# A two-layer graph network: one gather in eight waits for the second last one, and layer 2's dense terms are added a layer earlier

## The chip, the cores and the metric

The kernel runs on one core of a Trainium2 chip. A core has four compute engines with queues of their own: TensorE (PE, matrix products, with PEld for the loading of the stationary operand), VectorE (DVE), ScalarE (ACT) and GpSimd (POOL). SyncE (SP) issues plain transfers. Gathers, that is transfers whose source rows are given by a list of indices, are issued from POOL's queue. The metric is the device time of one execution in microseconds.

## The reference

The graph has 12,500 nodes with 128 features each and 200,000 edges, sorted by the node they end in. An edge's relation is the argmax of 10 of its 42 attributes. A layer takes, for every node and relation, the mean of the features of the source nodes, multiplies it by the relation's 128 x 128 matrix, sums over the relations, and adds the node's own features times a root matrix and a bias. Two such layers, with a relu between them, are followed by the residual and a layer norm:

```python
def _rgcn_layer(x, src, dst, edge_type, w_rel, root, bias):
    seg = dst * NUM_REL + edge_type
    xs = x[src]
    sums = jax.ops.segment_sum(xs, seg, num_segments=N * NUM_REL)
    cnt = jax.ops.segment_sum(jnp.ones(seg.shape, x.dtype), seg, num_segments=N * NUM_REL)
    mean = (sums / jnp.maximum(cnt, 1.0)[:, None]).reshape(N, NUM_REL, -1)
    return jnp.einsum('nrd,rdo->no', mean, w_rel) + x @ root + bias
h = jax.nn.relu(_rgcn_layer(x, src, dst, edge_type, w_rel1, root1, b1))
x = _layernorm(x + _rgcn_layer(h, src, dst, edge_type, w_rel2, root2, b2), axis=-1)
```

## The kernel before

The edges are cut into 1563 tiles of 128. For a tile, one gather (`gather`, L506 to L517) reads the 128 source rows from device memory into one sixteenth of the tile `g`: from `x` in layer 1, from `hD`, the hidden rows that layer 1 has stored, in layer 2. So a layer has 1563 gathers, the two layers 3126, and nothing else stands in POOL's queue once the constants are made. Sixteen tiles make a group, and `g` has three buffers, so gathers can be three groups ahead of their use. Towards the end of a layer the groups get smaller.

For each group, `ones` writes on DVE a matrix of zeros and weights per tile (`oh`, L531): its 120 columns are the 10 relations times 12 neighbouring end nodes, and a weight is one over the edge count of that node and relation. `sums` (L547) multiplies the gathered rows by it on PE into `zp` (L555); ACT moves the result to `zs` (L570). In full groups the first product of a group waits for all the group's gathers at once ("one wait per group"). `project` (L575) multiplies by the 10 relation matrices (L582). `add` (L593) spreads the result over 160 node columns (L598) and adds it on DVE into `acc` (L604), which holds 128 features x all nodes. `layer` (L606) is the loop over the groups: the projection stands one group, the addition two groups behind.

The nodes are cut into 29 blocks: 24 of 512, then smaller ones. When the groups have gone far enough that a block gets no more edges, its `finish` runs. In layer 1 that is `hidden` (L439): `block_in` (L402) has loaded the block's rows of `x` on SP's queue and transposed them (PE L415, ACT L417); `block_rows` (L422) forms in PSUM the root product (L427) plus the accumulator turned back to rows (L428), and writes layer 2's bias into the block's columns of `acc` (L430); then comes the relu and the store of the rows to `hD`. In layer 2 it is `final` (L449): `block_in` loads the block's rows of `x` and of `hD`, transposes the latter, `block_rows` adds root product and accumulator, DVE adds `x` (L458), then come mean and variance (L461, L462), the root (L464, L465), the normalised rows (L468) and the store to `out`.

In layer 1, work on the next 16,384 edges (argmax, edge counts, indices: `types`, `count`, `sources`) is done in steps between the groups. It shares the two PSUM buffers `ps_f` with `block_in`, `hidden` and `final`.

Layer 2's gathers follow layer 1's in the same queue. The first sixteen of them leave out the rows of the last two blocks, which are not stored yet; those edges are added from `late_h`, which is still in the core's memory (L544). If the input does not fit the assumptions (a flag, worked out in layer 2), a slow version under `tc.If` (L830) is run after it; its code calls `block_in`, `hidden` and `final` too.

Each gather has a semaphore out of eight, taken in turn (the trace numbers them 110 to 117). Before the kernel's change a gather waits for the one eight places ahead of it, which used the same semaphore; the first of a group also waits for the products that read its buffer. Where an instruction has more than one wait, a semaphore instruction stands ahead of it in the queue. `tc.add_manual_dep(a, b, ...)` makes instruction a come after b: with `whole` (a dependence on data) with a wait for b's completion, with `behind` in order only.

Of the kernel before, what the change touches and what calls it, by code (L numbers as in the profile page):

```python
# [9 lines left out]
F32 = mybir.dt.float32  # L10
BF16 = mybir.dt.bfloat16
I32 = mybir.dt.int32
AF = mybir.ActivationFunctionType
ALU = mybir.AluOpType
# [6 lines left out]
P = 128  # L21
# [8 lines left out]
HR = HT * WN  # L30
SW = 160
RING = 3
DB = 8
L = 40
CT = 128
YB = 512
# [7 lines left out]
def rgcn_resnorm_kernel(ctx: ExitStack, tc: tile.TileContext, x, src, dst, attr, w_rel1, root1, b1,  # L44
# [14 lines left out]
    nc = tc.nc  # L59
    N, C = x.shape  # L60
# [8 lines left out]
    t = NS * G  # L69
    while t < NT:  # L70
        n = NT - t
# [3 lines left out]
    NPAD = N + SW  # L75
    starts = list(range(0, N - YB - 2 * P, YB))
    starts += list(range(starts[-1] + YB, N, P))
    NBLK = len(starts)
# [15 lines left out]
    const = ctx.enter_context(tc.tile_pool(name="const", bufs=1))  # L94
    dram = ctx.enter_context(tc.tile_pool(name="dram", bufs=1, space=DRAM))
    fin = ctx.enter_context(tc.tile_pool(name="fin", bufs=1))
# [4 lines left out]
    hD = dram.tile([N, C], F32, name="hD")  # L101
# [57 lines left out]
    def then(engine, ins):  # L159

        if engine in loaded:
            loaded.remove(engine)
            tc.keep_in_program_order(ins)
        return ins
# [81 lines left out]
    k = 0  # L246
# [139 lines left out]
    def block(k):  # L386
        n0 = starts[k]
        n = (starts + [N])[k + 1] - n0
        return n0, n, [(t, min(P, n - t * P)) for t in range(-(-n // P))]

    def rows_dma(sb, dr, k, store):
        n0, n, _ = block(k)
        full = n // P
        pairs = []
        if full:
            pairs.append((sb[:, :full], dr[n0:n0 + full * P, :].rearrange("(t p) c -> p t c", p=P)))
        if n % P:
            pairs.append((sb[:n % P, full], dr[n0 + full * P:n0 + n, :]))
        for a, b in pairs:
            then("SP", nc.sync.dma_start(b, a) if store else nc.sync.dma_start(a, b))  # L400

    def block_in(k, l):  # L402

        n0, n, subs = block(k)
        last = "e" if k == NBLK - 1 else ""
        b = len(subs) if last else 4
        xb = fin.tile([P, b, C], F32, name="xb" + last)
        rows_dma(xb, x, k, False)
        fb = xb
        if l:  # L410
            fb = fin.tile([P, b, C], F32, name="hb" + last)
            rows_dma(fb, hD, k, False)
        pt = ps_f.tile([P, YB], F32, name="pf")
        for t, h in subs:
            nc.tensor.transpose(pt[:, t * P:t * P + h], fb[:h, t, :], ident[:h, :h])  # L415
        fT = fin.tile([P, b * P], F32, name="fT" + last)
        nc.scalar.activation(fT[:, :n], pt[:, :n], AF.Copy)  # L417
        return xb, fT

    zero = const.tile([P, YB], F32, name="zero")  # L420

    def block_rows(fT, k, l):  # L422

        n0, n, subs = block(k)
        pr = ps_f.tile([P, 4, C], F32, name="pf")
        for t, h in subs:
            nc.tensor.matmul(pr[:h, t, :], fT[:, t * P:t * P + h], rsb[l], start=True, stop=False)  # L427
            nc.tensor.matmul(pr[:h, t, :], acc[:, n0 + t * P:n0 + t * P + h], ident, start=False, stop=True)  # L428
        if l == 0:
            nc.scalar.activation(acc[:, n0:n0 + n], zero[:, :n], AF.Identity, bias=bsb[1])  # L430
        return pr

    def spans(k):
        n = block(k)[1]
        return [(p, slice(a, b)) for p, a, b in ((P, 0, n // P), (n % P, n // P, -(-n // P))) if p and b > a]

    anew = []

    def hidden(k, ready):  # L439

        xb, fT = ready
        pr = block_rows(fT, k, 0)
        i = k - (NBLK - 2)
        hb = late_h[:, i:i + 1] if i >= 0 and not anew else fin.tile([P, 4, C], F32, name="hb")
        for p, s in spans(k):
            nc.scalar.activation(hb[:p, s], pr[:p, s], AF.Relu)
        rows_dma(hb, hD, k, True)

    def final(k, ready):  # L449

        xb, fT = ready
        pr = block_rows(fT, k, 1)
        v = fin.tile([P, 4, C], F32, name="v")
        mv = small.tile([P, 4, 2], F32, name="mv")
        rstd = small.tile([P, 4], F32, name="rstd")
        _, n, subs = block(k)
        for p, s in spans(k):
            nc.vector.tensor_tensor(v[:p, s], pr[:p, s], xb[:p, s], op=ALU.add)  # L458
        for t, h in subs:
            st = small.tile([P, nc.vector.BN_STATS_DIM], F32, name="st")  # L460
            nc.vector.bn_stats(st[:h], v[:h, t, :])  # L461
            nc.vector.bn_aggr(mv[:h, t, :], st[:h])  # L462
        for p, s in spans(k):
            nc.scalar.activation(rstd[:p, s], mv[:p, s, 1], AF.Sqrt, bias=eps[:p])  # L464
            nc.vector.reciprocal(rstd[:p, s], rstd[:p, s])  # L465
        o = fin.tile([P, 4, C], F32, name="o")
        for t, h in subs:
            nc.vector.tensor_scalar(o[:h, t, :], v[:h, t, :], mv[:h, t, 0:1], rstd[:h, t:t + 1],  # L468
                                    op0=ALU.subtract, op1=ALU.mult)
        rows_dma(o, out, k, True)  # L470
# [9 lines left out]
    def head():  # L480
# [10 lines left out]
        for b in range(0, G, QB):  # L491
# [11 lines left out]
                nc.scalar.activation(late_w[i][:, b * KW:(b + QB) * KW], pm[i][:, :QB * KW], AF.Copy)  # L503
            yield

    def gather(table, t0, n):  # L506

        o = t0 % G
        if not o:
            shared["g"] = gpool.tile([P, G, C], F32, name="g")  # L510
        g = shared["g"][:, o:o + n]
        ix = idxE
        if is_head(table, t0):
            table, ix = table[:EARLY, :], idxH
        return g, [then("POOL", nc.gpsimd.indirect_dma_start(  # L515
            out=g[:, j, :], out_offset=None, in_=table, in_offset=bass.IndirectOffsetOnAxis(
                ap=ix[:, t0 + j:t0 + j + 1], axis=0))) for j in range(n)]  # L517

    whole = mybir.DependencyInfo(mybir.DependencyClass.Sync, mybir.DependencyReason.DATA)

    def halves(n):
        return [(h, min(HT, n - h * HT)) for h in range(-(-n // HT))]
# [83 lines left out]
    def layer(table, l, finish, steps, flag_too=False):  # L606

        done = 0
        held, projected = [], []
        ready = flag = given = made = None  # L610

        def project_oldest():
            projected.append(project(l, *held.pop(0)))

        def add_oldest():
            nonlocal done, given
            k, ms, at = projected.pop(0)
            add(k, ms, at)
            while done < NBLK and sum(groups[k]) >= done_after(done):
                finish(done, ready if done == NBLK - 1 else given or block_in(done, l))  # L620
                done += 1
                given = None

        for k in range(NG):
            end = k >= NS
            if k and not given and done < NBLK - 1:
                given = block_in(done, l)
            if projected:
                add_oldest()
            if end:  # L630

                if held:
                    project_oldest()
                    add_oldest()
                if not ready:
                    ready = block_in(NBLK - 1, l)
                    if flag_too:
                        loads, (flag,) = nc.values_load_multi_w_load_instructions(
                            flag_i[0:1, 0:1], min_val=0, max_val=1, skip_runtime_bounds_check_because=HELD)
                        for ld in loads:  # L640
                            tc.keep_in_program_order(ld)
                        loaded.update(("POOL", "DVE", "PE", "ACT", "SP"))
            held.append(sums(table, k, *(made or ones(k, table))))
            made = ones(k + 1, table) if end and k < NG - 1 else None
            if end or len(held) > 1:
                project_oldest()
            if end:
                add_oldest()
            if steps:
                till, left, s = steps[0]  # L650
                for _ in range(max(1, -(-left[0] // max(1, till - k)))):
                    left[0] -= 1
                    if next(s, steps) is steps:
                        steps.pop(0)
                        break
        while held or projected:
            if held:
                project_oldest()
            if projected:
                add_oldest()  # L660
        return flag
# [168 lines left out]
    with tc.If(flag > 0):  # L830
        nc.vector.memset(acc, 0.0)
        each_tile(lambda e, ty: relations(ty, BF16), [(g_count, None)])
        nc.sync.dma_start(counts, acc[:RS])
        for l, (table, finish) in enumerate(((x, hidden), (hD, final))):
            nc.vector.tensor_copy(acc, bsb[l].to_broadcast([P, NPAD]))
            each_tile(g_before(table), [(g_look, g_messages(l)), (g_add, None)])
            for k in range(NBLK):
                finish(k, block_in(k, l))
# [26 lines left out]
```

## Time and profile before

| | |
|---|---|
| median of 10 runs | 3937.04 us (3936.19 to 3937.81) |
| the profiled execution | 3937.68 us, span 3936.0 us |
| PE busy | 2358.7 us, 60% |
| DVE busy | 1504.9 us, 38% |
| ACT busy | 550.5 us, 14% |
| POOL busy | 2961.9 us, 75%, of it 3126 gathers of 0.947 us |
| transfers of POOL's queue (q0) | 205.07 MB, 19.8% of the 16 engines' span |
| transfers of SP's queue (q1) | 71.03 MB, 5.7% |
| granted PE clock | 0.779 of full speed |

The page gives each engine's busy time, a chain of work followed back from the last instruction, and groups of instructions by line. L515 is the line of the gathers. For a gather POOL is busy while it writes the transfer's descriptors; the transfer lands later, and the trace records when its semaphore has its full count. "issue" is idle time in which the engine waited for nothing that the profile shows. In lists of instructions in order of time a row has the start, the duration, engine, line and operation, and in brackets the idle time ahead of it with what ended it.

### The profile page before, as it was taken

How to read it: one execution, taken by the hardware profiler on the slowest of the kernel's cores; microseconds unless marked ns; L12 is line 12 of the kernel's file. 1: busy time of each engine (PE TensorE's matmuls, PEld its weight loads, DVE VectorE, ACT ScalarE, POOL GpSimd, SP SyncE). 2: the span in 40 equal slices, each digit the busy share in tenths (PEclk: the TensorE clock that was granted, in tenths of full speed). 3: DMA queues.
4: the chain of work that ended last, by engine and by line, in shares of the span. 5: the costliest groups of instructions: out<-in, count | busy, mean ns of one | idle time of the engine just before them, and what ended most of it. 6: DMA issues, size and time to landing. Idle time of an engine off the chain costs nothing.

```text
span 3936.0 us, 43878 instructions
## 1 busy us (share of the span) xinstructions
PE 2358.7 (60%) x16242; PEld 2262.4 (57%) x16242; DVE 1504.9 (38%) x4623; ACT 550.5 (14%) x1177; POOL 2961.9 (75%) x3142
## 2 busy tenths in 40 slices
PE   4656556565666656667755565565555565566556
PEld 3655555565555555556745565555555555555556
DVE  6444434343444444443423333333323333333333
ACT  2111111111111111111211111111111111111111
POOL 7777777777777777777777777777777777777776
PEclk8777777787777777778877777777777777777778
DMA  5322323223223222222222222222222222222222
GB/s 164 89 74 75 95 60 89 88 67 89 73 76 90 62 88 62 63 64 57 68 60 59 61 69 61 61 61 64 67 61 61 61 69 61 61 61 69 61 60 57
DMA packets 180540, 278.99 MB, mean 71 GB/s; under 512 B 55610, under 2 KB 127177, under 8 KB 177193
## 3 DMA queue, kind: packets, MB, share of 16 engines
q0 software_dynamic: 100032, 205.07, 19.8%
q1 hardware_dynamic: 78577, 71.03, 5.7%
q8 instruction: 132, 2.16, 0.2%
q14 instruction: 89, 0.73, 0.1%
q10 hardware_dynamic: 1710, 0.01, 0.0%
HBM read 262.28 MB, written 13.60 MB: 70 GB/s over the span
## 4 chain that ended last, share of the span: by engine, by line
POOL 68%; issue 26%; DMA 3%; PE 2%; ACT 0%; DVE 0%; POOLq 0%; ACTq 0%
POOL g L515 68%; DMA g<-in_x_dram,idxE 2%; PE pp L582 1%; DMA g<-hD,idxE 1%; PE zp L555 1%; ACT zs L570 0%; PE pp L598 0%; PE pf L428 0%; DVE oh L531 0%; DMA g<-hD,idxH 0%; PE pf L427 0%; DVE acc L604 0%; ACT rstd L464 0%; ACT ms L588 0%; DVE o L468 0%
## 5 line engine op out<-in xcount | busy, mean ns | idle before, releaser
L555 PE MATMUL zp<-oh,g 128*128 128x120 f32 x6252 | 1128.2, 355 | 1504.4 <-DMA g<-hD,idxE 784.4
L555 PEld LDWEIGHTS zp<-oh,g 128*128 128x128 f32 x6252 | 1086.4, 268 | 1545.0 <-issue 1489.4
L515 POOL DMA_INDIRECT g<-in_x_dram,idxE x1563 | 1480.8, 947 | 477.2 <-issue 469.8
L515 POOL DMA_INDIRECT g<-hD,idxE x1547 | 1463.3, 946 | 471.7 <-issue 466.8
L531 DVE TENSOR_SCALAR oh<-bank,keyE,wE 128x120 f32<-128x120 f32 x3110 | 997.7, 392 | 764.5 <-PE zp L555 764.2
L582 PE MATMUL pp<-w,zs 128*96 128x128 f32 x7840 | 901.6, 274 | 21.8 <-ACT zs L570 19.1
L582 PEld LDWEIGHTS pp<-w,zs 128*96 128x96 f32 x7840 | 871.9, 164 | 27.6 <-ACT zs L570 23.6
L570 ACT ACTIVATE zs<-zp 128x480 f32<-128x480 f32 (+1 forms) x782 | 383.4, 575 | 2121.8 <-PE zp L555 2105.6
L604 DVE TENSOR_TENSOR acc<-acc,pp 128x160 f32 x202 | 64.3, 319 | 1359.8 <-PE pp L598 1345.8
L598 PE MATMUL pp<-at,ms 96*128 96x160 f32 (+2 forms) x784 | 210.3, 408 | 6.2 <-ACT ms L588 4.7
L598 PEld LDWEIGHTS pp<-at,ms 96*128 96x128 f32 (+2 forms) x784 | 170.9, 272 | 21.9 <-ACT ms L588 15.7
L588 ACT ACTIVATE ms<-pp 96x256 f32<-96x256 f32 (+1 forms) x198 | 74.5, 376 | 459.1 <-PE pp L582 459.1
L535 DVE TENSOR_SCALAR at<-bank,place 96x160 f32<-96x160 f32 x392 | 130.5, 371 | 0.0
L370 DVE TENSOR_TENSOR eqb<-pf,kh 128x1344 bf16<-128x1344 f32 (+2 forms) x65 | 100.2, 1550 | 67.9 <-PE pf L374 58.9
L428 PE MATMUL pf<-ident,acc 128*128 128x128 f32 x392 | 93.2, 327 | 0.7 <-DVE acc L604 0.6
L427 PE MATMUL pf<-root,fT 128*128 128x128 f32 x388 | 88.5, 316 | 0.8 <-ACT fT L417 0.5
L428 PEld LDWEIGHTS pf<-ident,acc 128*128 128x128 f32 x392 | 77.1, 244 | 1.6 <-DVE acc L604 1.6
L427 PEld LDWEIGHTS pf<-root,fT 128*128 128x128 f32 x388 | 72.8, 233 | 1.8 <-ACT fT L417 1.4
L430 ACT ACTIVATE acc<-zero,b 128x512 f32<-128x512 f32 (+2 forms) x29 | 19.0, 655 | 328.3 <-PE pf L428 328.3
L464 ACT ACTIVATE rstd<-mv,eps 128x4 f32<-128x4 f32 (+2 forms) x29 | 8.6, 297 | 371.7 <-DVE mv L462 371.6
L372 PE MATMUL pf<-eqb,identb 128*128 128x512 bf16 (+2 forms) x130 | 50.5, 389 | 12.8 <-DVE eqb L370 12.8
L374 PE MATMUL pf<-eqb,identb 128*128 128x512 bf16 (+2 forms) x130 | 50.9, 391 | 0.0
(121 smaller groups left out, 510.5 us busy)
## 6 DMA issues: line engine op xcount, KB each, us to landing
m<-in_edge_attr_dram SPq DMA_DIRECT2D x24, 1344.0 KB
g<-in_x_dram,idxE POOLq DMA_INDIRECT x1563
g<-hD,idxE POOLq DMA_INDIRECT x1547
xb<-in_x_dram SPq DMA_DIRECT2D x46, 256.0 KB
hD<-hb SPq DMA_DIRECT2D x23, 256.0 KB
hb<-hD SPq DMA_DIRECT2D x23, 256.0 KB
out_dram<-o SPq DMA_DIRECT2D x23, 256.0 KB
w<-in_L_gnn_w_rel_dram SPq DMA_DIRECT2D x2, 640.0 KB
```

Of the source, the lines that this page charges most:

```text
L370: nc.vector.tensor_tensor(eq[:p], kp[:p, None, :R].to_broadcast([p, DB, R]), fore, op=ALU.is_equal)
L427: nc.tensor.matmul(pr[:h, t, :], fT[:, t * P:t * P + h], rsb[l], start=True, stop=False)
L428: nc.tensor.matmul(pr[:h, t, :], acc[:, n0 + t * P:n0 + t * P + h], ident, start=False, stop=True)
L515: return g, [then("POOL", nc.gpsimd.indirect_dma_start(out=g[:, j, :], out_offset=None, in_=table, in_offset=bass.IndirectOffsetOnAxis(ap= ...
L531: then("DVE", nc.vector.tensor_scalar(oh[:, j, :], iotaP[:, :KW], keyE[:, t:t + 1], w[:, t:t + 1], op0=ALU.is_equal, op1=ALU.mult))
L535: nc.vector.tensor_scalar(at[:, h, :], iotaP[:HR], place[:, h, k:k + 1], None, op0=ALU.is_equal)
L555: m = nc.tensor.matmul(zp[:, j // QB, j % QB * KW:(j % QB + 1) * KW], g[:, j, :], oh[:, j, :], start=not is_head(table, t0), stop=not is_h ...
L570: then("ACT", nc.scalar.activation(zs[:, :, b * QB:b * QB + m, :], zp[:, b, :m * KW].rearrange("c (j r n) -> c r j n", r=NREL, n=WN), AF.C ...
L582: nc.tensor.matmul(po[:m * WN, h], zs[:, r, h * HT:h * HT + m].rearrange("c j n -> c (j n)"), wsb[l][:, r, :], start=(r == 0), stop=(r == ...
L588: nc.scalar.activation(ms[:, :n // HT], po[:HR, :n // HT], AF.Copy)
L598: nc.tensor.matmul(pa, ms[:m * WN, h], at[:m * WN, h], start=(h == 0), stop=(h == len(parts) - 1))
L604: nc.vector.tensor_tensor(acc[:, s], acc[:, s], pa, op=ALU.add)
```

## The change

Two things are changed. First, the gathers are put in a fixed order, and of each eight the seventh (tile number 6 modulo 8) gets a wait for the completion of the gather two places ahead of it. Second, layer 2's dense terms go into its accumulators in layer 1: when a block's hidden rows are made, they are transposed at once, multiplied by layer 2's root matrix, and written with layer 2's bias and the transposed `x` (which is there for layer 1's root product) into the block's columns of `acc`. `final` then only turns the accumulator back to rows in PSUM and normalises from there; layer 2 loads neither `x` nor `hD` by blocks.

```diff
+PACE = 8
...
     def block_in(k, l):
 
+        if l:
+            return None
...
-        fb = xb
-        if l:
-            fb = fin.tile([P, b, C], F32, name="hb" + last)
-            rows_dma(fb, hD, k, False)
...
-        if l == 0:
-            nc.scalar.activation(acc[:, n0:n0 + n], zero[:, :n], AF.Identity, bias=bsb[1])
...
+    def hidden(k, fT):
...
+            nc.tensor.matmul(pr[:h, t, :], fT[:, t * P:t * P + h], rsb[0], start=True, stop=False)
             nc.tensor.matmul(pr[:h, t, :], acc[:, n0 + t * P:n0 + t * P + h], ident, start=False, stop=True)
...
             nc.scalar.activation(hb[:p, s], pr[:p, s], AF.Relu)
         rows_dma(hb, hD, k, True)
+        pt = ps_f.tile([P, YB], F32, name="pf")
+        for t, h in subs:
+            nc.tensor.transpose(pt[:, t * P:t * P + h], hb[:h, t, :], ident[:h, :h])
+        hT = fin.tile([P, YB], F32, name="hT")
+        nc.scalar.activation(hT[:, :n], pt[:, :n], AF.Copy)
+        po = ps_f.tile([P, YB], F32, name="pf")
+        nc.tensor.matmul(po[:, :n], rsb[1], hT[:, :n], start=True, stop=True)
+        nc.vector.scalar_tensor_tensor(acc[:, n0:n0 + n], po[:, :n], bsb[1], fT[:, :n], op0=ALU.add, op1=ALU.add)
...
-        v = fin.tile([P, 4, C], F32, name="v")
+        v = ps_f.tile([P, 4, C], F32, name="pf")
...
-        for p, s in spans(k):
-            nc.vector.tensor_tensor(v[:p, s], pr[:p, s], xb[:p, s], op=ALU.add)
+        for t, h in subs:
+            nc.tensor.matmul(v[:h, t, :], acc[:, n0 + t * P:n0 + t * P + h], ident, start=True, stop=True)
...
+    begun = []
...
+        for j in range(n):
+            d = then("POOL", nc.gpsimd.indirect_dma_start(
+                out=g[:, j, :], out_offset=None, in_=table, in_offset=bass.IndirectOffsetOnAxis(
+                    ap=ix[:, t0 + j:t0 + j + 1], axis=0)))
+            if (t0 + j) % PACE == PACE - 2 and len(begun) > 1:
+
+                tc.add_manual_dep(d.ins, begun[-2].ins.name, whole, reason="no more than two under way")
+            if begun:
+                tc.add_manual_dep(d.ins, begun[-1].ins.name, behind, reason="gathers in their order")
+            begun.append(d)
+        return g, begun[-n:]
```

More of the change, by code (lines that the diff above doesn't have):

```diff
@@ L400, in rows_dma @@
             then("SP", nc.sync.dma_start(b, a) if store else nc.sync.dma_start(a, b))
+    zero = const.tile([P, YB], F32, name="zero")
     def block_in(k, l):
+        if l:
+            return None
         n0, n, subs = block(k)
@@ L408, in block_in @@
         rows_dma(xb, x, k, False)
-        fb = xb
-        if l:
-            fb = fin.tile([P, b, C], F32, name="hb" + last)
-            rows_dma(fb, hD, k, False)
         pt = ps_f.tile([P, YB], F32, name="pf")
         for t, h in subs:
-            nc.tensor.transpose(pt[:, t * P:t * P + h], fb[:h, t, :], ident[:h, :h])
+            nc.tensor.transpose(pt[:, t * P:t * P + h], xb[:h, t, :], ident[:h, :h])
         fT = fin.tile([P, b * P], F32, name="fT" + last)
         nc.scalar.activation(fT[:, :n], pt[:, :n], AF.Copy)
[L418 to L428, printed above, removed]
-        if l == 0:
-            nc.scalar.activation(acc[:, n0:n0 + n], zero[:, :n], AF.Identity, bias=bsb[1])
-        return pr
+        return fT
+    anew = []
     def spans(k):
@@ L437, in rgcn_resnorm_kernel @@
     anew = []
-    def hidden(k, ready):
-        xb, fT = ready
-        pr = block_rows(fT, k, 0)
+    def hidden(k, fT):
+        n0, n, subs = block(k)
+        pr = ps_f.tile([P, 4, C], F32, name="pf")
+        for t, h in subs:
+            nc.tensor.matmul(pr[:h, t, :], fT[:, t * P:t * P + h], rsb[0], start=True, stop=False)
+            nc.tensor.matmul(pr[:h, t, :], acc[:, n0 + t * P:n0 + t * P + h], ident, start=False, stop=True)
         i = k - (NBLK - 2)
@@ L447, in hidden, with final @@
         rows_dma(hb, hD, k, True)
-    def final(k, ready):
-        xb, fT = ready
-        pr = block_rows(fT, k, 1)
-        v = fin.tile([P, 4, C], F32, name="v")
+        pt = ps_f.tile([P, YB], F32, name="pf")
[6 more added lines that the diff above has]
+        nc.vector.scalar_tensor_tensor(acc[:, n0:n0 + n], po[:, :n], bsb[1], fT[:, :n], op0=ALU.add, op1=ALU.add)
+    def final(k, _):
+        n0, n, subs = block(k)
+        v = ps_f.tile([P, 4, C], F32, name="pf")
         mv = small.tile([P, 4, 2], F32, name="mv")
         rstd = small.tile([P, 4], F32, name="rstd")
-        _, n, subs = block(k)
-        for p, s in spans(k):
-            nc.vector.tensor_tensor(v[:p, s], pr[:p, s], xb[:p, s], op=ALU.add)
+        for t, h in subs:
+            nc.tensor.matmul(v[:h, t, :], acc[:, n0 + t * P:n0 + t * P + h], ident, start=True, stop=True)
         for t, h in subs:
@@ L504, in head @@
             yield
+    begun = []
+    whole = mybir.DependencyInfo(mybir.DependencyClass.Sync, mybir.DependencyReason.DATA)
     def gather(table, t0, n):
@@ L514, in gather @@
             table, ix = table[:EARLY, :], idxH
[L515 to L519, printed above, removed]
+        for j in range(n):
[8 more added lines that the diff above has]
+        return g, begun[-n:]
     def halves(n):
@@ L619, in add_oldest @@
             while done < NBLK and sum(groups[k]) >= done_after(done):
-                finish(done, ready if done == NBLK - 1 else given or block_in(done, l))
+                finish(done, *(ready if done == NBLK - 1 else given or (block_in(done, l),)))
                 done += 1
@@ L626, in layer @@
             if k and not given and done < NBLK - 1:
-                given = block_in(done, l)
+                given = (block_in(done, l),)
             if projected:
@@ L635, in layer @@
                 if not ready:
-                    ready = block_in(NBLK - 1, l)
+                    ready = (block_in(NBLK - 1, l),)
                     if flag_too:
@@ L834, in rgcn_resnorm_kernel @@
         for l, (table, finish) in enumerate(((x, hidden), (hD, final))):
-            nc.vector.tensor_copy(acc, bsb[l].to_broadcast([P, NPAD]))
+            if not l:
+                nc.vector.tensor_copy(acc, bsb[l].to_broadcast([P, NPAD]))
             each_tile(g_before(table), [(g_look, g_messages(l)), (g_add, None)])
```

## The prediction

> **What bounds the kernel now.** I read the page's busy times first, then the chain that ended last, then the waits, then the gathers in order of time, and last the places where a gather's landing is seen.
>
> ```profile
> span 3936.0 us, 43878 instructions
> PE 2358.7 (60%) x16242; PEld 2262.4 (57%) x16242; DVE 1504.9 (38%) x4623; ACT 550.5 (14%) x1177; POOL 2961.9 (75%) x3142
> ...
> POOL 68%; issue 26%; DMA 3%; PE 2%; ACT 0%; DVE 0%; POOLq 0%; ACTq 0%
> ```
>
> POOL is busiest at 75%, and the chain is POOL for 68% and "issue" for 26%. The waits say what that issue is:
>
> ```profile
> POOL g L515 <- issue: 941.5, 3088, 0.3
> ...
> POOL g L515 <- DMA g<-in_x_dram,idxE: 5.5, 18, 0.3
> POOL g L515 <- DMA g<-hD,idxE: 4.9, 16, 0.3
> POOL g L515 <- DVE idxE L173: 0.9, 1, 0.9
> ```
>
> 941.5 us in 3088 gaps is 0.305 us each: a fixed gap behind every gather, never above 0.3. A gather lasts 0.947 us, so one begins every 1.252 us, and 3126 x 1.252 = 3913 us of the 3936. Nothing that POOL waits for has ever cost it more than that gap, except the first index. The other engines only follow: PE stands idle 6 to 11 us in each group of sixteen gathers (20 us).
>
> What matters for this change is when a gather is complete. The first lines below are from the gathers in order of time, the others from the chain:
>
> ```profile
> 4.31 1.16 POOL L515 DMA_INDIRECT g<-in_x_dram,idxE  x1 [0.92 <-DVE idxE L173]
> 5.77 0.94 POOL L515 DMA_INDIRECT g<-in_x_dram,idxE  x1 [0.30 <-issue]
> 7.02 0.95 POOL L515 DMA_INDIRECT g<-in_x_dram,idxE  x1 [0.30 <-issue]
> ```
>
> ```profile
> 3012.25 2.45 DMA g<-hD,idxE
> 3014.75 0.95 POOL g L515
> ```
>
> ```profile
> 455.67 6.03 DMA g<-in_x_dram,idxE
> 461.70 0.02 issue
> 461.72 0.02 POOLq L515
> ```
>
> The gather begun at 3012.25 was complete 2.45 us later; two gathers later POOL began the next one at 3014.75, 2.50 us after it. So "second last complete" is true just about when the gather would begin anyway. The gather begun at 455.67 needed 6.03 us. The trace's landing records (the last of the sixteen counts that each gather's semaphore gets, less the gather's start) give all of them: of 3117, a tenth land within 2.46 us, half within 2.53, a quarter after 2.58, a tenth after 3.08, 345 after 3.0, the longest after 7.92. The long ones lie beside loads and stores that SP has issued.
>
> **The change: the paced gathers.** Gathers 6, 14, 22 ... of each layer's 1563 get a wait: 195 a layer, 390 in all. The wait stands in POOL's queue, so every later gather is behind it, then PE's group, then the rest. POOL has no other work in the layers and is on the chain all the time, and the gap after a late gather in the trace is again 0.30, so what a wait costs is not made up. A paced gather is late by landing + h - 2.502 where that is positive; h is the time from the landing to the start of the gather. No row shows h with POOL waiting. Bounds: 0; 0.135, the median by which PE's sums follow the landing of their last gather; 0.29, the first gather, the only one that truly waited: DVE wrote its index until 4.02, it began at 4.31. I take 0.29, since it is the same instruction on the same engine, and PE's own start after a DVE result (3.09 to 3.21, s_f) is 0.12, near its 0.135 after a landing, so the releaser does not make the difference. The sequencer side agrees: its semaphore instruction stands 0.02 behind the landing above.
>
> Mean lateness over all landings (so that no chance position counts), times 195: with h = 0.29, layer 1 109.3 us, layer 2 76.9 us, together 186.2. Of this the median landing alone makes 62.3 + 60.9; the rest is the tail of late landings. With h = 0.135 it is 79.1 + 46.6 = 125.7; with h = 0 it is 54.6 + 22.4 = 77.0. Upper end: the first gather also lasted 1.16 us in place of 0.95; if every gather that finds the queue empty does, 390 x 0.21 = 82 us more, 268.
>
> Each paced gather needs two waits (its own semaphore's last use eight gathers back, and the new one), so it gets a semaphore instruction on POOL's sequencer, as the 198 at group starts have (17 ns each); today the sequencer runs about six gathers ahead of them, with the wait it does not, and this lies within h. The fixed order of the gathers is the order they have now: nothing.
>
> **A rule against the row.** The trace has the second last gather landing 2.45 us after it begins, at the median 2.53. The Trainium skill, "DMA: Bandwidth & Descriptors", section on the anatomy of one DMA, fits about 2.0 us plus bytes over 436 GB/s for a DMA from POOL: 2.15 us for these 64 KB. By that, the typical landing with h = 0.29 would stay below 2.50 and only the late tail would cost, about 67 us by an estimate from that page. The measured landings decide. The same page's rules for kernel authors (overlap DMA with compute: issue early, wait late) speak against a wait set right behind the issue.
>
> **The change: layer 2's terms moved into layer 1.** Per block (29 blocks, 98 row tiles) layer 1 gains: transposes of the new rows (four, 0.60 us on PE), their copy on ACT (0.60), a root product of 512 columns (nearest row: two 480-column products, 0.97) and one DVE addition (nearest: v, 0.69). It loses the bias write on ACT (19.0 us in all, 0.655 each). So PE gets about 1.6 us and some 1.4 us of standing behind ACT in each block, one block in four groups, 80 us, against 6 to 11 us of idle time in each group. The gather buffers give a second cover: three groups of 20 us, so PE may be over 20 us late before POOL feels it. Cost: nothing; with both covers gone 29 x 3 = 87 us. The moved work also takes turns in two PSUM buffers with the index and count work, and the next chunk's index must be ready: at 618.5 for gathers at 644. A few us of delay fit in.
>
> Layer 2 loses, on SP's queue, 28 + 1 loads of hD and of x each; on PE 98 transposes and 98 root products; on ACT 29 copies; on DVE 29 additions. All of it is beside the gathers, but the loads make landings late: late landings next to x and hD loads in layer 2 come to some 50 us of lateness over 1563 gathers, an eighth of which would fall on paced ones: -6 us. SP's store of the hidden rows stands before the moved work, and layer 2's first gather of late rows has 7 us to spare (stores in at 1974.6, gather at 1981.6): nothing.
>
> At the end, after the last gather (3915.29), the last block goes add 3928.00, acc into PSUM 3928.38, v 3928.86, statistics 3929.18. The v addition (0.29 and its hand-over) goes; the readers take PSUM: -0.4 us. Bounds: 0 and -0.5.
>
> **Sum.** 3936.0 + 186.2 - 6 - 0.4 = 4115.8 span; the profiled execution took 3937.68, 1.7 beside its span: 4117.5. It lay 0.6 above the median of the ten runs (3937.04): 4117.
>
> **Rivals.**
> (A) Covered wait: the paced gather is dispatched at its usual time and only late landings count (h = 0): 3936.0 + 77 - 6 + 1 = about 4008. For it: the median landing misses the natural start by 0.03 us only. Against: every start on POOL after a real wait in the trace came 0.16 us or more after its release.
> (B) Restart: the gather after an empty queue lasts 1.16 us as the first did: 4117 + 82 = 4199. Against: the first is also the first use of its code, and another early gather (12.02, 1.28 us) was long in a full queue.
> (C) The other side: the 0.30 us gap behind each gather depends on how many are under way, and draining the queue shortens it. It decides at 180 us over the 2736 unpaced gathers: 0.066 us each, gap 0.305 down to 0.239. Gap at 0.20: 2736 x 0.105 = 287 us gained, 3937 + 180 - 287 = 3830. Against: the second gather, with only one before it, already shows 0.30 at 5.77; nothing in the trace shows a shorter one.
> (D) The wait is not made, as something waited for already implies it: only the end moves, 3936.6. Against: each gather's own wait is on the one eight back, which says nothing of the one two back.
>
> **How the numbers follow.** Forecast 0.50; A 0.22; B 0.10; C 0.12; D 0.06. Slower: forecast, A and B, 0.82; same: D; faster: C. The measurement cannot tell less than 0.2% (8 us) from no change. The range holds the forecast, A and B, 0.82 together: from a little below A, 3988, as the tail of late landings may be smaller once POOL pauses, to B with a few us on top, 4205.
>
> **What would show it.** In the profile after: POOL's busy time unchanged near 2962; idle time before paced gathers released by a gather's DMA, near 0.58 us typically (0.305 + 0.28) and some of several us; a cadence of 1.25 between the others; the chain with some 5% DMA on g; no x or hD loads in layer 2. Wrong if the gap of unpaced gathers is not 0.30, if gathers after a wait last longer than 0.95, or if POOL waits for an index or for PE.

## The result and the profile after

The changed kernel takes 4202.73 us (median of 8 runs, 4192.98 to 4213.64) against 3937.0 for the kernel before (median of 28): a ratio of 1.0674, with a 95% interval of 1.0665 to 1.0684. The forecast was 4117 us with a range of 3988 to 4205. The profiled execution took 4197.48 us, with a span of 4195.8, 259.8 us more than before. The runs also spread over 20.7 us, where the 28 of the kernel before lay within 2.1.

The page of the changed kernel, its busy times and its chain:

```profile
span 4195.8 us, 43813 instructions
PE 2416.8 (58%) x16104; PEld 2240.6 (53%) x16104; DVE 1509.5 (36%) x4623; ACT 535.3 (13%) x1148; POOL 2961.2 (71%) x3142
...
POOL 50%; issue 28%; DMA 20%; PE 2%; DVE 0%; POOLq 0%; ACT 0%; ACTq 0%
```

POOL is busy for the same time as before (2961.2 us; it was 2961.9) and works no more slowly. A fifth of the chain is now transfers, which were 3% of it. The waits of POOL, with total, count and longest:

```profile
POOL g L518 <- issue: 844.7, 2714, 3.7
POOL g L518 <- DMA g<-hD,idxE: 204.3, 189, 1.8
POOL g L518 <- DMA g<-in_x_dram,idxE: 163.5, 216, 4.3
```

The gathers from `hD`, that is layer 2, wait for more time in fewer waits than those of layer 1, although their longest wait is shorter. That was not forecast. The 3.7 us in the first row is also a paced gather of layer 2, of which more below. The gathers in order of time in layer 2 show the pattern of eight: seven gaps of 0.30 us, then one of about a microsecond:

```profile
2988.89 0.95 POOL L518 DMA_INDIRECT g<-hD,idxE  x1 [0.30 <-issue]
2990.95 0.95 POOL L518 DMA_INDIRECT g<-hD,idxE  x1 [1.11 <-DMA g<-hD,idxE]
2992.20 0.95 POOL L518 DMA_INDIRECT g<-hD,idxE  x1 [0.30 <-issue]
```

The chain in order of time tells why. First a paced gather of layer 1, then one of layer 2:

```profile
1320.70 2.47 DMA g<-in_x_dram,idxE
1323.17 0.26 issue
1323.43 0.94 POOL g L518
```

```profile
3009.19 2.54 DMA g<-hD,idxE
3011.73 0.03 issue
3011.75 0.02 POOLq L518
3011.77 0.69 issue
3012.47 0.27 POOL g L518
```

In layer 1 the gather starts 0.26 us after the landing it waits for. In layer 2 a semaphore instruction of POOL's sequencer (POOLq) ends 0.04 us after the landing, and the gather starts only 0.69 us after that. From landing to start it is 0.258 to 0.260 us for all 195 paced gathers of layer 1, and 0.736 to 0.738 for 191 of the 195 of layer 2. The other four of layer 2, each 424 gathers after the last, start 3.32 us after their landing. One of them in the chain:

```profile
2389.06 2.56 DMA g<-hD,idxE
2391.62 0.02 issue
2391.65 0.02 POOLq L518
2391.66 3.28 issue
2394.94 0.95 POOL g L518
```

The semaphore instruction ends as soon after the landing as elsewhere, and then POOL stands for 3.28 us and not 0.69. What it does in that time is open.

Both kinds have two waits, one for the semaphore's own last use eight gathers back and the new one. Each of these gathers carries one; the other goes into the semaphore instruction ahead of it (198 of these on L515 before, 587 on L518 after). In layer 1 the paced gather has semaphore 116 and itself waits for 114, the new one; the semaphore instruction ahead holds the wait for 116, long satisfied. A layer has 1563 gathers, which is 3 modulo 8, so in layer 2 the paced gather has semaphore 111: there the gather holds the wait for 111, and the semaphore instruction the new one, for 117. In every pair seen the gather holds the lower number. That the number decides is not shown by this: where the first gather of a group has three waits, the semaphore instruction holds 110 and 101 and the gather 109.

**Where the 259.8 us went.** I take as lateness of a gather the idle time ahead of it less the usual 0.305 us. Paced gathers: 98.7 us in layer 1, 161.9 in layer 2, of it 10 us from the four that start 3.32 us after the landing. Six other gathers, three in each layer and 424 apart there, were 0.26 us late in layer 1 and about 1.0 in layer 2: 3.9 us. All gathers together were shorter by 0.9. The first began 0.1 earlier. From the start of the last gather to the end it is 17.04 us, where it was 20.66: -3.6. The sum is 98.7 + 161.9 + 3.9 - 0.9 - 0.1 - 3.6 = 259.9. No other gather waited for PE, DVE or ACT, so the moved dense terms cost POOL nothing in this execution.

### The profile page after: what moved, and what is told of

Its sections match the earlier page's. It is cut to its first block, busy times and chain, and to the rows that moved or that the text cites. A ratio compares the mean times of both kernels' runs of the same rounds, so it can differ in the third digit from the quotient of the medians.

```text
span 4195.8 us, 43813 instructions
## 1 busy us (share of the span) xinstructions
PE 2416.8 (58%) x16104; PEld 2240.6 (53%) x16104; DVE 1509.5 (36%) x4623; ACT 535.3 (13%) x1148; POOL 2961.2 (71%) x3142
## 3 DMA queue, kind: packets, MB, share of 16 engines
q8 instruction: 131, 2.15, 0.2%
## 4 chain that ended last, share of the span: by engine, by line
POOL 50%; issue 28%; DMA 20%; PE 2%; DVE 0%; POOLq 0%; ACT 0%; ACTq 0%
POOL g L518 50%; DMA g<-hD,idxE 12%; DMA g<-in_x_dram,idxE 8%; PE zp L563 1%; PE pp L590 1%; POOLq L518 0%; DMA g<-hD,idxH 0%; PE pp L606 0%; PE pf L447 0%; DVE eqb L371 0%; ACT zs L578 0%; DMA s_i<-in_src_dram 0%; PE pf L435 0%; PE pf L443 0%; PE pf L434 0%
## 5 line engine op out<-in xcount | busy, mean ns | idle before, releaser
L563 PE MATMUL zp<-oh,g 128*128 128x120 f32 x6252 | 1154.7, 367 | 1519.5 <-DMA g<-hD,idxE 783.2
L563 PEld LDWEIGHTS zp<-oh,g 128*128 128x128 f32 x6252 | 1118.7, 280 | 1575.7 <-issue 1507.4
L518 POOL DMA_INDIRECT g<-hD,idxE x1547 | 1462.7, 946 | 634.8 <-issue 430.2
L518 POOL DMA_INDIRECT g<-in_x_dram,idxE x1563 | 1480.5, 947 | 576.3 <-issue 410.2
L590 PE MATMUL pp<-w,zs 128*96 128x128 f32 x7840 | 926.9, 276 | 129.9 <-ACT zs L578 118.1
L606 PE MATMUL pp<-at,ms 96*128 96x160 f32 (+2 forms) x784 | 162.8, 330 | 67.5 <-ACT ms L596 66.5
L606 PEld LDWEIGHTS pp<-at,ms 96*128 96x128 f32 (+2 forms) x784 | 117.2, 195 | 110.2 <-ACT ms L596 105.5
L371 DVE TENSOR_TENSOR eqb<-pf,kh 128x1344 bf16<-128x1344 f32 (+2 forms) x65 | 98.7, 1546 | 32.8 <-PE pf L375 24.3
L448 DVE SCALAR_TENSOR_TENSOR acc<-pf,b,fT 128x512 f32<-128x512 f32 (+1 forms) x28 | 19.0, 679 | 150.6 <-PE pf L447 150.6
L435 PE MATMUL pf<-ident,acc 128*128 128x128 f32 x196 | 41.4, 295 | 4.1 <-DVE acc L612 4.1
L434 PE MATMUL pf<-root,fT 128*128 128x128 f32 x194 | 39.6, 287 | 0.6 <-ACT fT L418 0.6
L457 PE MATMUL pf<-ident,acc 128*128 128x128 f32 x196 | 33.2, 289 | 10.8 <-DVE acc L612 10.8
L435 PEld LDWEIGHTS pf<-ident,acc 128*128 128x128 f32 x196 | 32.0, 205 | 8.9 <-DVE acc L612 8.7
L447 PE MATMUL pf<-hT,root 128*128 128x512 f32 (+2 forms) x58 | 35.7, 704 | 1.0 <-ACT hT L445 0.9
```

The costliest lines, as they stand in the source:

```text
L371: nc.vector.tensor_tensor(eq[:p], kp[:p, None, :R].to_broadcast([p, DB, R]), fore, op=ALU.is_equal)
L518: d = then("POOL", nc.gpsimd.indirect_dma_start(out=g[:, j, :], out_offset=None, in_=table, in_offset=bass.IndirectOffsetOnAxis(ap=ix[:, t ...
L563: m = nc.tensor.matmul(zp[:, j // QB, j % QB * KW:(j % QB + 1) * KW], g[:, j, :], oh[:, j, :], start=not is_head(table, t0), stop=not is_h ...
L590: nc.tensor.matmul(po[:m * WN, h], zs[:, r, h * HT:h * HT + m].rearrange("c j n -> c (j n)"), wsb[l][:, r, :], start=(r == 0), stop=(r == ...
L606: nc.tensor.matmul(pa, ms[:m * WN, h], at[:m * WN, h], start=(h == 0), stop=(h == len(parts) - 1))
```

## The experiments

Theory 1: the whole loss is the wait, the moved terms are free. Theory 2: which of its two places a wait has, 0.26 or 0.74 us after the landing, goes with the pair of semaphores. The rivals: the moved work bears part of the loss; layer 2, or gathers from `hD`, are slow to restart as such; a wait has its price even where it is covered.

One thing has to be known to read all of what follows. Beside these runs the kernel before took not 3937 us but between 4680 and 4797. There is no trace of it from there; in the traces of the runs beside it PE stood still for stretches of some 20 us, and POOL waited for PE. A stretch that stands still and one that does not, from the run dense_early (PE, PEld, DVE, ACT and POOL busy, granted clock, DMA share, GB/s):

```profile
2980.00:3002.00 22.00, 2.97 (x8) 1.87 (x8) 4.14 (x14) 1.10 (x3) 14.42 (x16) 0.50 0.19 48
3005.00:3016.00 11.00, 11.00 (x77) 11.00 (x76) 5.71 (x19) 1.96 (x4) 3.66 (x4) 0.76 0.07 18
```

In the first stretch the granted clock is 0.50, and PE makes 8 products in 22 us, where the second has 77 in 11. So the totals of these runs cannot be set against 3937 and 4203. What can be read are the gaps of single gathers, since the two causes lie at different places: POOL waits for PE only at the first gather of a group, where a buffer must be free, and for the landing of a gather only at paced ones. Below, both are given as lateness.

**1. No wait, the moved terms alone (dense_early, dense_early_b, dense_early_c).**

```diff
-            if (t0 + j) % PACE == PACE - 2 and len(begun) > 1:
-
-                tc.add_manual_dep(d.ins, begun[-2].ins.name, whole, reason="no more than two under way")
```

> The changed kernel without the new wait: the order of the gathers and the early dense terms stay. Theory 1 (the whole loss is the wait): about 3936.5 us, between 3933 and 3937.5, that is 0 to 0.1% under the kernel before; every gap between gathers is back at 0.305 us, and layer 2 has no loads of x and hD by blocks. Rival (part of the loss is the moved work: PE late, an index late, PSUM buffers held): above 3945 us, with idle time of POOL released by PE or DVE in layer 1.

> The same kernel as dense_early, once more, as the kernel before took 4688 us beside the first try and not 3937: there PE stood still between single instructions and POOL waited for PE. Where the kernel before takes about 3937 us: theory 1 expects 3933 to 3937.5 us; the rival (the moved work bears part of the loss) above 3945. Where it takes about 4690 again, nothing can be said of a kernel that POOL bounds.

> The same kernel as dense_early, on a chip on which the kernel before takes about 3937 us, if there is one: theory 1 (the whole loss is the wait) expects 3933 to 3937.5 us, the rival (the moved work bears part of the loss) above 3945.

Measured: 4769.2 us beside 4687.8 (ratio 1.0174, 1.0160 to 1.0188), 4814.1 beside 4777.5 (1.0082, 1.0060 to 1.0103), 4803.6 beside 4749.5 (1.0100, 1.0072 to 1.0128). Every gather but the first of each group keeps its gap of 0.305 (one or two in each run are 0.26 late); the lateness at the first ones is 804, 830 and 848 us. The numbers forecast were for a kernel that POOL bounds, and none of these is one. So they neither support nor refute theory 1 as a total. Where PE is held back, the moved terms and the fixed order together cost some 1 to 2%; what in them does it was not found.

**2. The wait alone (pace_only).** The changed `gather`, with its wait and its order, in the kernel before; nothing else.

> The kernel before with the new wait alone. Theory 1: about 4207 us (4195 to 4220): the loss of the changed kernel (266 us), and up to 6 us more, since layer 2's loads are still there and make landings late. Rival (moved work bears part of it): clearly under 4195 us.

Measured: 4735.95 us beside 4687.8, 1.0095 (1.0080 to 1.0111). Paced gathers are late by 90 us in layer 1 and 169 in layer 2 without any moved term, near the 98.7 and 161.9 of the changed kernel. So the lateness is the wait's. The total moved by 48 us only. The profiled execution is the slowest of the five, 104 us above the kernel before, with 259 us of paced lateness; in it the first gathers of groups are late by 570 us, where dense_early has 804. That fits pauses in which PE catches up, so that POOL waits less for it later; it was not shown apart.

**3. The same semaphores in both layers (same_sem, same_sem_c).**

```diff
-            if (t0 + j) % PACE == PACE - 2 and len(begun) > 1:
+            if len(begun) % PACE == PACE - 2:
```

> The changed kernel with its paced gathers counted through both layers, so that in layer 2 too the paced gather has the semaphore 116 and waits for 114, as in layer 1 (in the changed kernel layer 2 has 111 waiting for 117). Theory 2 (a start comes 0.258 us after the landing if the new wait is in the gather itself, 0.738 us if it is in the semaphore instruction ahead of it; which of the two depends on the numbers of the semaphores): layer 2's lateness falls from 162 to about 65 us, the time from 4203 to about 4106 (4095 to 4117). Rival (gathers from hD, or layer 2, are slow to restart as such): 4203, unchanged, start after landing still 0.738 in layer 2.

> The same kernel as same_sem. Where the kernel before takes about 3937 us: theory 2 expects about 4106 us (4095 to 4117), as layer 2's paced gathers then start 0.258 us after the landing and not 0.738; the rival (layer 2 as such is slow) 4203. The first try showed the 0.258 already in the gaps, beside PE stalls that hid it in the total.

Measured: 4857.9 us beside 4687.8 (1.0346, 1.0299 to 1.0394) and 4806.5 beside 4749.5 (1.0103, 1.0076 to 1.0130). The forecast of 4106 could not be met or missed here. The lateness of layer 2's paced gathers is 77 and 80 us (65 were forecast), where pace_only beside it has 169 and wrap_sem (experiment 4), with the moved terms too, 170; in layer 1 it is 88 and 75. The total does not follow: same_sem has the least paced lateness of the three, 165 us against 259 and 326, and takes the longest. One paced gather of layer 2 in same_sem, and one in pace_only:

```profile
3038.22 0.94 POOL L518 DMA_INDIRECT g<-hD,idxE  x1 [0.30 <-issue]
3039.72 0.94 POOL L518 DMA_INDIRECT g<-hD,idxE  x1 [0.56 <-DMA g<-hD,idxE]
```

```profile
3035.33 0.94 POOL L520 DMA_INDIRECT g<-hD,idxE  x1 [0.30 <-issue]
3037.39 0.95 POOL L520 DMA_INDIRECT g<-hD,idxE  x1 [1.12 <-DMA g<-hD,idxE]
```

The edit changes only which gathers are paced, and with that the numbers of their semaphores, and takes away about half a microsecond at each in layer 2. The four gathers that start 3.32 us after a landing in the changed kernel have gaps of 3.6 to 3.7 in pace_only; in same_sem they are not paced, and their gap is 0.30. That gathers from `hD` or layer 2 as such restart slowly is refuted.

**4. The other pair of semaphores in both layers (wrap_sem).**

```diff
-            if (t0 + j) % PACE == PACE - 2 and len(begun) > 1:
+            if len(begun) > 1 and len(begun) % PACE == 1:
```

> The changed kernel with its paced gathers counted through both layers at the second of eight, so that the paced gather has semaphore 111 and waits for 117 in both layers. Theory 2: layer 1 now has 0.738 us too, its lateness goes from 98 to about 190 us, the time to about 4295 (4280 to 4310). Rival (layer 2 as such is slow): layer 1 stays at 0.258 us, 4203 unchanged. What I forecast on record (0.29 us everywhere) would give about 4117.

Measured: 4805.0 us beside 4687.8, 1.0268 (1.0241 to 1.0296). Now layer 1 pays too: its paced gathers are late by 157 us (190 were forecast), layer 2's by 170, and the typical idle time ahead of a paced gather in layer 1 is 1.08 us, where pace_only and same_sem have 0.61. Half of layer 1's paced gathers follow the first of a group directly, and where that one waited for PE, the landing was in by then; the other half alone have 115 us. Experiments 3 and 4 turn the price off in layer 2 and on in layer 1, so it goes with the pair of semaphores, and with it the place of the late wait, and not with the layer. What else decides the place of a wait was not tried.

**5. Waiting for the third last (third_last).**

```diff
-            if (t0 + j) % PACE == PACE - 2 and len(begun) > 1:
-
-                tc.add_manual_dep(d.ins, begun[-2].ins.name, whole, reason="no more than two under way")
+            if (t0 + j) % PACE == PACE - 2 and len(begun) > 2:
+
+                tc.add_manual_dep(d.ins, begun[-3].ins.name, whole, reason="no more than two under way")
```

> The changed kernel with the wait on the third last gather. Three gathers take 3.754 us, a landing 2.53 typically. Theory 2 (0.258 us after the landing in layer 1, where the wait for 113 is in the gather; 0.738 in layer 2, where the wait for 116 is in the semaphore instruction): the typical wait is covered (2.53 + 0.738 = 3.27), only late landings cost, 18 to 23 us in layer 1 and 5 to 7 in layer 2, so about 3963 us (3950 to 3975). Rival (each wait has a price of its own, covered or not: 0.26 to 0.74 us, 390 times): 4130 or more.

Measured: 4807.8 us beside 4777.5, 1.0060 (1.0034 to 1.0085). The paced gathers are late by 13.9 us in layer 1 and 13.3 in layer 2, together 27 where 23 to 30 were forecast. The split was not met: 18 to 23 and 5 to 7 were forecast, and in layer 2 four gathers, the same four as above, make 9 of the 13 us, with gaps of 2.4 to 2.8. An ordinary paced gather shows a gap of 0.30. So a wait has no price of its own: with one more gather between, even the slow place is covered, and only late landings and those four are left.

**6. Lighter kernels (light_before, light_dense, light_after, light_same_sem).** Four kernels with one relation product in place of ten, to free PE:

```diff
-            for r in range(NREL):
-                nc.tensor.matmul(po[:m * WN, h], zs[:, r, h * HT:h * HT + m].rearrange("c j n -> c (j n)"),
-                                 wsb[l][:, r, :], start=(r == 0), stop=(r == NREL - 1))
+            nc.tensor.matmul(po[:m * WN, h], zs[:, 0, h * HT:h * HT + m].rearrange("c j n -> c (j n)"),
+                             wsb[l][:, 0, :], start=True, stop=True)
```

> The kernel before with nine of the ten relation products (L582) left out, so that its output lacks nine relations' terms; PE's work per full group falls from about 12 to about 8 us. On this chip the full kernel takes about 4750 us, since PE stands still between its instructions. If that is PE's work alone, the gathers bound this one again: 3925 to 3940 us. If it stays over 4000, PE still holds POOL back.

> The changed kernel without its wait, with the same nine of ten relation products left out. Theory 1 (the moved work costs nothing where POOL bounds): as light_before within 4 us, rather under it. Rival (the moved work makes POOL wait): more than 8 us over light_before, with POOL's first gathers of groups late.

> The changed kernel with the same nine of ten relation products left out. Theory 1 and 2: light_before plus 260 us (250 to 275), of it about 97 in layer 1 (0.258 us from landing to start) and 162 in layer 2 (0.738).

> light_after with the paced gathers counted through both layers (semaphore 116 waits for 114 in both). Theory 2: light_before plus 163 us (150 to 175), 97 less than light_after. Rival (layer 2 as such): as light_after.

Measured: 4711.0, 4708.4, 4599.3 and 4579.4 us, beside 4687.5 of the full kernel before. The output of all four lacks nine relations' terms. The purpose was missed: with nine tenths of the relation products gone PE still holds POOL back, its granted clock is 0.64 where the full kernels had 0.73 to 0.74, and the first gathers of groups are late by 766 us in light_before and 764 in light_dense. The times of these two agree within 3 us, so here the moved terms cost nothing. light_after and light_same_sem show the two prices once more: layer 2's paced gathers are late by 154 and 48 us. Layer 1's are late by 67 and 82 with the same code there, so single executions differ by some 15 us. The totals go against the forecast: light_after is 109 us faster than light_dense, as its first gathers are late by 443 us only, and light_same_sem is 20 us below it where 97 were forecast. Why 221 us of pauses save some 320 us of waiting for PE is open.

## Why the prediction was right, and where it was not

**The place and the sign.** The forecast said that the wait stands in POOL's queue, that POOL is on the chain all the time, that the second last gather lands just when the next would begin, and that nothing makes it up. The profile after shows all four, with the gaps of 0.30 unchanged between the others. The time lies inside the range, 86 us above the forecast and at its upper edge; four of the eight runs lie above that edge. The edge was set by rival B, whose mechanism did not occur, so that the median still falls inside is luck. The chain has 20% transfers where some 5% was forecast: a landing that is waited for stands on the chain with its whole length, as the rows of 2.47 and 2.54 us show.

**The term that was mis-sized: h.** The forecast took one h, 0.29 us, for both layers, 109.3 + 76.9 us. With the measured h and the landings of the trace of before, the same sum gives 103 us in layer 1 (h = 0.258) and 164 in layer 2 (h = 0.738); measured were 98.7 and 161.9, the latter 152 without the excess of the four odd gathers. So the method and layer 1 were right, and layer 2's h was too small by 0.45 us and lay outside the bounds of 0 to 0.29. The step that failed is the sentence that the semaphore instruction on POOL's sequencer "lies within h". It does where it holds the old wait and not where it holds the new one, which fits a sequencer that hands the gather over only once that wait is met; the rows show the order, not the reason. The Trainium skill, "Perfetto Trace Analysis", section on identifying dependency chains, says that an instruction waiting on several engines may get semaphore instructions with further waits ahead of it. This trace has 587 of them, most for transfers of POOL's own queue; the price here, 0.48 us, does not stand there.

**The landings.** That the awaited landing takes 2.53 us and not 2.15 decided the case: the trace of after has the same median. By the 2.15 us that follow from the Trainium skill, "DMA: Bandwidth & Descriptors", section on the anatomy of one DMA, an ordinary paced gather of layer 2 would by an estimate be late by 0.39 us; the typical one is late by 0.75. (The tail alone, which the prediction put at 67 us by that figure, comes to 63 over the landings of before, all taken 0.38 us shorter.)

**Rival A (covered wait)** falls: no paced gather began earlier than 0.258 us after its landing. **Rival B (restart)** falls, although its 4199 us came closest: gathers after a wait last 0.946 us at the median, like the others. **Rival C (a shorter gap)** falls in the profile after, with 0.305 for the unpaced gathers. **Rival D (no wait made)** falls: all 390 paced gathers start late.

**The moved terms.** Nothing on POOL in layer 1, as forecast, in the one profile that POOL bounds; a run of them alone under that bound was not had, so the total is not shown apart. The -6 us for the loads taken out of layer 2 is not shown. Late landings are rarer, a tenth after 2.63 us in layer 2, where it was 2.80; but in layer 1, which lost no loads, they are rarer too (3.14, where it was 3.33), and pace_only, which keeps the loads, has the same lateness in layer 2 as wrap_sem, 169 and 170 us.

**The end.** The forecast was -0.4 us, measured -3.6. Before, PE was behind at the end:

```profile
3915.29 0.95 POOL L515 DMA_INDIRECT g<-hD,idxE  x1 [0.31 <-issue]
...
3918.37 2.38 PE L582 MATMUL pp<-w,zs 128*48 128x128 f32 x20 [0.72 <-ACT zs L570]
...
3924.65 2.42 PE L582 MATMUL pp<-w,zs 128*84 128x128 f32 x20 [1.26 <-ACT zs L570]
```

After, PE waits for the last landing and goes on at once. The last gather, the sums that its landing releases and the last group's projection, in order of time:

```profile
4178.73 0.94 POOL L518 DMA_INDIRECT g<-hD,idxE  x1 [0.30 <-issue]
...
4181.22 0.48 PE L563 MATMUL zp<-oh,g 128*128 128x120 f32 x2 [0.64 <-DMA g<-hD,idxE]
...
4182.97 4.03 PE L590 MATMUL pp<-w,zs 128*84 128x128 f32 x20 [1.26 <-ACT zs L578]
```

The last group's projection begins 9.4 us after the last gather before, and 4.2 us after it now; it then takes 1.6 us longer for the same 20 products, for which no cause was looked for. From its end to the end of the kernel it is 8.75 us, where it was 8.88: the step that was forecast, -0.4 us, measured -0.1. The forecast looked only at the chain behind the last sum and not at PE's queue. How much of the earlier projection is due to the missing root products and how much to the pause at 4173.7 is not separated.

## What to carry to other kernels

A wait on a queue that bounds the kernel is priced by the landing of what it waits for, less the time that the queue needs to get there, plus the way from the landing to the start; with landings of 2.53 us and a cadence of 1.25, waiting for the second last cost 261 us in 390 waits, and waiting for the third last 27 (the latter measured beside PE's standstills). Where an instruction gets two waits, see which of the two is the late one: in the instruction itself it cost 0.26 us here, in a semaphore instruction ahead of it 0.74, and which of the two it was went with the pair of semaphores. A mean over all landings of the kernel before was enough to size such a wait to within some 8%, once the h measured afterwards was put in.

## What the runs showed of the hardware that was not expected

- A gather starts 0.69 us after a late semaphore instruction of POOL's sequencer; with one more gather between, as in third_last, the same pair costs nothing (a gap of 0.30).
- At steps of 424 gathers single ones are late for no dependence that the trace shows: in the changed kernel three unpaced ones by 0.26 us in layer 1, three by about 1.0 in layer 2, and four paced ones of layer 2 start 3.32 us after their landing. The last kind also stands in pace_only, wrap_sem and light_after at the same four gathers, and not in same_sem, where these four are not paced. Counted through both layers, all ten of the changed kernel lie whole multiples of 106 gathers apart. The cause is open.
- PE's standstills: a granted clock of 0.50 over 22 us with 8 products, single products 0.7 to 1.4 us after their weight loads, while the gathers kept their 1.25 us. With fewer products the mean clock fell further, from about 0.74 to 0.64.
- In that regime pauses on POOL are partly or wholly given back: in the profiled execution of pace_only 259 us of paced lateness stand against 104 us over the kernel before. The wait alone cost 0.95% there by the medians; the whole change costs 6.7% where POOL bounds.
